# A two-layer graph kernel: a second queue fetches whole tiles of rows, 16 of them, for layer 1

## The chip, the cores and the metric

The kernel runs on one core of one Trainium2 chip. The metric is the device time of one execution in microseconds (us), as the median of several executions. A difference of less than 0.2%, about 7 us here, can't be told from no change.

## The reference

There are 12,500 nodes with 128 features each and 200,000 edges, sorted by their target node; every edge has one of 8 relations. Two layers are computed, and then a layer norm of the sum with the input:

```python
def _rgcn_conv(x, src, dst, et, basis, comp, root, bias):
    W = jnp.einsum('rb,bio->rio', comp, basis)
    xw = jnp.einsum('ni,rio->nro', x, W)
    msgs = xw[src, et]
    seg = dst * N_REL + et
    summed = jax.ops.segment_sum(msgs, seg, num_segments=N_NODES * N_REL)
    cnt = jax.ops.segment_sum(jnp.ones((msgs.shape[0],), x.dtype), seg, num_segments=N_NODES * N_REL)
    mean = summed / jnp.maximum(cnt, 1.0)[:, None]
    agg = mean.reshape(N_NODES, N_REL, HIDDEN).sum(axis=1)
    return agg + x @ root + bias
...
for l in range(N_LAYERS):
    h = jax.nn.relu(_rgcn_conv(h, src, dst, edge_type, basis[l], comp[l], root[l], bias[l])) + h
...
x = _layernorm(x + h, axis=-1)
```

## The kernel before

The edges are cut into 1,563 tiles of 128, and eight tiles make a quad; there are 196 quads. One turn of the main loop handles one quad, and the variable `o` counts the turns. The code numbers the layers 0 and 1; the text says layer 1 and layer 2. Nothing in the order of instructions is decided at run time: the program writes one list of operations, each engine takes its own in that order, and a wait is set where an operation needs the result or the buffer of another engine's.

Layer 1 first sums the rows of x by target and relation and multiplies by the weights afterwards. In turn `o` the following is written, in this order:

- GpSimd (POOL) fetches the rows of quad `o + 5`: one indirect DMA for each tile, 128 rows of 512 bytes (`gather`, line 806). The quads land in a ring of seven buffers `rows`, so the fetch of quad q + 7 has to wait until TensorE has read quad q. For the last six quads of the layer the fetch is only two turns ahead.
- TensorE (PE) multiplies each tile of rows with a one-hot matrix `dm` that VectorE (DVE) made: 16 instructions, line 1364, into the two banks `s` (`means`). Called M here.
- ScalarE (ACT) copies what is left from the turn before (`batch`, all at line 704): table halves (`y_row` out of the banks `pt` and `ct`), then the last product (`ys` out of `y`), then the new sums (`sT` out of `s`, two instructions). Behind them it issues stores that are due (`h_d`, `y_d`, line 701).
- `single_lists` and `single_rows` (lines 728 to 767) come next, see below.
- VectorE makes the one-hot matrices of quad `o + 2` and whatever other work is due.
- TensorE multiplies `sT` of quad `o - 1` with the eight relations' weights (`product`, line 1396, called P), adds the result into the accumulator of a node block (`place`, lines 1427 and 1429), and works on what else is due.

Three kinds of other work share the turns. In turns 0 to 42 the edge lists are turned and counted. From turn 50 on a table of h times the weights of layer 2 is made for every finished node block of 128 (`table`, line 1495, two halves a block). While more than four halves are waiting, one is made and copied by ScalarE within the turn (called T1), before TensorE may use the bank `pt` again for the next one (T2); a third, T3, goes to the bank `ct`. T2 and T3 are copied in the next turn's `batch`. By the program's lists the backlog is 51 halves at turn 50 and 6 at turn 75; after that T1 is made in the turns 76 to 80, 84 and 92. In turns 96 to 161 edges of layer 2 are sorted into groups on VectorE and TensorE with small copies and stores on ScalarE (`lo_d`, `sc_d`), and only one table half a turn is made; a backlog of 22 halves left by then goes in turns 162 to 176, again with T1 in each. Until turn 49 ScalarE copies `ys` in the same turn as P.

Layer 2 fetches rows of that table `y_d` by the same kind of indirect DMA, 1,067 tiles and 62 others; its fetches stand behind layer 1's in GpSimd's list, and the third quad of layer 2 waits until all of the table has been stored.

Some tiles of layer 1 aren't fetched by GpSimd. The list `SINGLES` names them: an issuing engine, the layer, and the tiles. Now there is one entry, SyncE's (SP) queue with every 56th tile from 191 on, 24 tiles. For such a tile the queue's engine issues 128 plain DMAs, one for each row. It does so in eight chunks of 16. In front of every second chunk it loads 32 row addresses from a list in memory into registers; the list `off_d` is written once, in turn 14, by one DMA of single 4-byte words. Every chunk has its place in the order of the turns (`single_rows`), before the turn that sums the tile:

```python
if (t - ts.step - 2 * Q + c * ts.step * RC // P) // Q != o:
    continue
...
return [by[e].dma_start(b[c * RC + j:c * RC + j + 1, :], bass.AP(
    tensor=t8.tensor, offset=offsets[e][a + j], ap=[[4 * D, 1], [1, 4 * D]]))
    for j in range(RC)]
```

Each engine in the list has two tile buffers `hw_<engine>`. GpSimd's `gather` leaves such tiles out, and M reads them from those buffers.

Of the kernel before, what the change touches and what calls it, by code (L numbers as in the profile page):

```python
# [430 lines left out]
def ordered_path(  # L431
# [38 lines left out]
    Q = 8  # L470
    NQ = -(-T // Q)
# [38 lines left out]
    NR = len(ROUTED)  # L510
    SORT = 96
    RC, RL = 16, 32
    SINGLES = [("SP", 0, range(191, NQ * Q - 80, 56))]
    SINGLE = {(l, t): (i, k) for i, (_, l, ts) in enumerate(SINGLES) for k, t in enumerate(ts)}
    LISTED = (14, NQ - 24)
    assert all(l == 0 or all(t // Q not in ROUTED and t // Q < NQ - 4 for t in ts) for _, l, ts in SINGLES)
    assert len(SINGLE) == sum(len(ts) for _, _, ts in SINGLES)
    assert D == P and R * K == P and B == BF + 1 and 1 < TL and LAST < P and BF % 4 == 0 and Q == G and N % 2 == 0
# [8 lines left out]
    def keep(shape, dtype, name):  # L527
        return const.tile(shape, dtype, name=name)
# [147 lines left out]

    hw_b = {e: [keep([P, D], F32, f"hw_{e}{i}") for i in range(2)] for e in {e: 0 for e, _, _ in SINGLES}}
    offs = [keep([P, len(ts)], I32, f"off{i}") for i, (_, _, ts) in enumerate(SINGLES)]
    off_d = [dram.tile([len(ts), P], I32, name=f"off_d{i}") for i, (_, _, ts) in enumerate(SINGLES)]
    by = {"SP": nc.sync, "ACT": nc.scalar}  # L680
# [1865 lines left out]
def kernel(  # L2546
# [18 lines left out]
    flag = ctx.enter_context(tc.tile_pool(name="flag", bufs=1))  # L2565
    bad = flag.tile([1, 1], I32, name="bad")
    plan = ordered_path(tc, bad, x, src, dst, et, basis, comp, root, bias, out)
    every = [mybir.EngineType.PE, mybir.EngineType.Activation, mybir.EngineType.DVE, mybir.EngineType.Pool,
             mybir.EngineType.SP]
# [36 lines left out]
```

## Time and profile before

| What | Value |
|---|---|
| time, median of 3 | 3384.41 us (3383.34 to 3385.06) |
| the profiled execution, its own time | 3385.05 us |
| its span, first to last instruction | 3383.1 us |
| granted TensorE clock, mean | 0.911 |
| PE busy | 2766.1 us (82%) |
| POOL busy | 2547.9 us (75%) |
| DVE busy | 2270.8 us (67%) |
| ACT busy | 644.9 us (19%) |
| layer 1's fetches on POOL | 4.6 to 1949.4 us |
| layer 2's fetches on POOL | 1950.6 to 3363.7 us |

Issuing a DMA isn't counted as busy time, so SP has no row here, and ACT's 19% holds only its copies. PE's busy time holds matmuls at both of its clock rates. A queue's issuing shows in rows that carry SPq, ACTq or POOLq.

### The profile page before, as it was taken

What the parts mean: (1) busy time and instruction counts of PE and PEld (TensorE: products, weight loads), DVE (VectorE), ACT (ScalarE), POOL (GpSimd) and SP (SyncE); (2) the same over time, 40 slices, a digit from 0 to 9 for tenths busy, and PEclk for the clock granted to TensorE, in tenths of its full rate; (3) what the DMA queues carried; (4) which work ended last, traced back from release to release, by engine and by line L of the source; (5) the groups of instructions that cost most, each with busy time, mean ns of one, the idle gap of its engine ahead of it and who ended that gap; (6) DMA issues with size and microseconds to landing.
All of it is one profiled execution on the core that took longest, in us unless ns stands there. A gap on an engine that the chain in (4) does not pass through costs nothing.

```text
span 3383.1 us, 73915 instructions
## 1 busy us (share of the span) xinstructions
PE 2766.1 (82%) x27537; PEld 2228.2 (66%) x27537; DVE 2270.8 (67%) x6302; ACT 644.9 (19%) x1627; POOL 2547.9 (75%) x2677
## 2 busy tenths in 40 slices
PE   6777667877667777777776739999999999999995
PEld 4565565656566666766565627777777777777774
DVE  6665454463367888888333238888888888888884
ACT  1211112222122222222222211111111111111110
POOL 7777777777777777777777777777777777777775
PEclk8999879888888888888988879999999999999997
DMA  4242223443322232222333232233223322333222
GB/s 138 56 59 64 57 77 113 132 130 95 89 82 81 75 89 76 82 77 82 115 105 89 88 101 73 72 84 85 78 78 84 84 78 78 84 85 82 78 78 61
DMA packets 171649, 289.03 MB, mean 85 GB/s; under 512 B 66163, under 2 KB 102813, under 8 KB 171285
## 3 DMA queue, kind: packets, MB, share of 16 engines
q0 software_dynamic: 85408, 175.09, 20.3%
q1 hardware_dynamic: 47146, 50.19, 5.0%
q10 hardware_dynamic: 38731, 58.99, 4.9%
q8 instruction: 218, 3.57, 0.5%
q14 instruction: 146, 1.20, 0.1%
HBM read 218.35 MB, written 65.70 MB: 84 GB/s over the span
## 4 chain that ended last, share of the span: by engine, by line
PE 43%; POOL 40%; issue 13%; DVE 2%; DMA 2%; ACT 1%; POOLq 0%; ACTq 0%; SPq 0%; DVEq 0%
POOL rows L806 40%; PE pt L1918 11%; PE y L1938 9%; PE po L1938 7%; PE po L1958 3%; PE s L2059 3%; PE ct L2026 2%; PE s L1364 2%; PE y L1396 1%; DMA rows<-in_x_dram,idx 1%; PE s L2061 1%; DVE dm L1270 1%; PE s L2063 1%; DVE arena L999 1%; PE pt L1495 0%
## 5 line engine op out<-in xcount | busy, mean ns | idle before, releaser
L806 POOL DMA_INDIRECT rows<-in_x_dram,idx x1539 | 1476.8, 960 | 471.3 <-issue 463.5
L806 POOL DMA_INDIRECT rows<-y_d,idy x1067 | 1010.4, 947 | 325.1 <-issue 316.6
L1364 PE MATMUL s<-dm,rows 128*128 128x128 f32 x3078 | 531.6, 344 | 379.6 <-DMA rows<-in_x_dram,idx 351.8
L1364 PEld LDWEIGHTS s<-dm,rows 128*128 128x128 f32 x3078 | 495.2, 252 | 441.1 <-issue 228.1
L1270 DVE TENSOR_SCALAR dm<-cols,kr,w 128x128 f32<-128x128 f16 x1563 | 525.1, 400 | 194.7 <-PE pt L1495 54.8
L1396 PE MATMUL y<-w_sb,sT 128*128 128x128 f32 x3136 | 438.6, 299 | 46.4 <-ACT sT L704 46.4
L1396 PEld LDWEIGHTS y<-w_sb,sT 128*128 128x128 f32 x3136 | 424.6, 217 | 56.4 <-ACT sT L704 55.2
L1918 PE MATMUL pt<-arena,dm 128*32 128x128 f32 x12152 | 391.3, 275 | 2.8 <-DVE dm L1868 2.1
L704 ACT ACTIVATE sT<-s 128x512 f32<-128x512 f32 x391 | 212.3, 594 | 824.8 <-PE s L1364 824.8
L1918 PEld LDWEIGHTS pt<-arena,dm 128*32 128x32 f32 x12152 | 324.6, 110 | 55.2 <-issue 43.0
L1938 PE MATMUL y<-arena,dm 128*128 128x304 f32 x620 | 229.6, 452 | 35.1 <-DVE arena L1885 35.1
L1229 DVE TENSOR_SCALAR sT<-cols,kr,w 128x32 f32<-128x32 f16 x1040 | 238.1, 300 | 7.4 <-PE s L2063 7.3
L1868 DVE TENSOR_TENSOR dm<-arena,cols 128x768 f32<-128x768 f16 x248 | 231.3, 933 | 4.1 <-DMA dm<-sc_d 3.7
L1448 DVE TENSOR_TENSOR po<-po,carry 128x128 f32<-128x128 f32 x98 | 28.8, 294 | 296.9 <-PE pt L1495 104.2
L1938 PE MATMUL po<-arena,dm 128*128 128x304 f32 x620 | 210.3, 421 | 0.0
L704 ACT ACTIVATE dm<-pt 128x256 f32<-128x256 f32 x248 | 95.4, 385 | 578.2 <-PE pt L1918 533.6
L1495 PE MATMUL pt<-w_sb,arena 128*128 128x512 f32 (+1 forms) x326 | 174.5, 618 | 26.3 <-ACT y_row L704 14.9
L704 ACT ACTIVATE y_row<-pt 128x512 f32<-128x512 f32 x165 | 98.5, 597 | 417.8 <-PE pt L1495 153.3
L1938 PEld LDWEIGHTS y<-arena,dm 128*128 128x128 f32 x620 | 102.9, 189 | 88.4 <-DVE arena L1885 35.3
L1885 DVE TENSOR_SCALAR arena<-cols,comp_sb 128x608 f32<-128x608 f16 x155 | 134.9, 902 | 36.1 <-DMA arena<-y_d,arena 36.0
L1938 PEld LDWEIGHTS po<-arena,dm 128*128 128x128 f32 x620 | 118.4, 191 | 41.3 <-issue 0.7
L1885 DVE TENSOR_SCALAR arena<-cols,sel 128x608 f32<-128x608 f16 x155 | 134.8, 902 | 0.0
(327 smaller groups left out, 3583.5 us busy)
## 6 DMA issues: line engine op xcount, KB each, us to landing
hw_SP<-in_x_dram SPq DMA_DIRECT2D x3072, 0.5 KB
y_d<-y_row ACTq DMA_DIRECT2D x96, 512.0 KB
rows<-in_x_dram,idx POOLq DMA_INDIRECT x1539
rows<-y_d,idy POOLq DMA_INDIRECT x1067
arena<-lo_d SPq DMA_DIRECT2D x62, 256.0 KB
x_g<-in_x_dram SPq DMA_DIRECT2D x24, 512.0 KB
h_d<-arena ACTq DMA_DIRECT2D x96, 64.0 KB
out_dram<-x_g SPq DMA_DIRECT2D x12, 512.0 KB
```

The lines of the kernel that those rows point to most:

```text
L704: act(lambda: nc.scalar.activation(out_t, in_t, AF.Copy), reads, writes)
L806: ins.append(nc.gpsimd.indirect_dma_start(out=t[:, i - q * Q, :], out_offset=None, in_=table_t, in_offset=bass.IndirectOffsetOnAxis(ap=ids ...
L1229: vec(in_turn([lambda i=i: nc.vector.tensor_scalar(t[:, i, :], cols[:, :2 * K], kr[:, i0 + i:i0 + i + 1], w[:, i0 + i:i0 + i + 1], op0=ALU ...
L1270: emits.append(lambda i=i: nc.vector.tensor_scalar(t[:, i - q * Q, :wide], cols[:, :wide], ids[:, i:i + 1], w[:, i:i + 1], op0=ALU.is_equa ...
L1364: last = nc.tensor.matmul(s_b[i // 4][0][:, i % 4, :], t[:, i, :] if one is None else one[0], d[:, i, :], start=True, stop=True)
L1396: last = nc.tensor.matmul(y[:m], t[:, r, :nt, :].rearrange("p t k -> p (t k)"), w_sb[:, 0, r, :], start=(r == 0), stop=(r == R - 1))
L1495: pe(lambda: nc.tensor.matmul(hb[:n].rearrange("p r d -> p (r d)"), hT[:, j * P:j * P + n], w_sb[:, 1, k * H:(k + 1) * H, :].rearrange("p ...
L1868: emits = [lambda: nc.vector.tensor_tensor(o[:, :3 * n].rearrange("p (j c) -> p j c", j=3), bits[:, None, u * n:(u + 1) * n].to_broadcast( ...
L1885: vec(lambda v=v, o=o: nc.vector.tensor_scalar(o, segs_p, sg[:, v:v + 1], sg[:, NTL + v:NTL + v + 1], op0=ALU.is_equal, op1=ALU.mult), ["n ...
L1918: last = nc.tensor.matmul(b[k * CAP:(k + 1) * CAP, x, :], o[:n, c:c + CAP], hT[:n, j * P:(j + 1) * P], start=jj == 0, stop=jj == SIZE[g] - 1)
L1938: last = nc.tensor.matmul(b.rearrange("p t d -> p (t d)")[:, :SEG], g[:, x * P:(x + 1) * P], o[:, k * SEG:(k + 1) * SEG], start=v == 0, st ...
L1958: pe(in_turn([lambda r=r: nc.tensor.matmul(b[:NW, 0, :], t_s[:, r * NW:(r + 1) * NW], w_sb[:, 1, r, :], start=r == 0, stop=r == R - 1) for ...
```

## The change

`SINGLES` gets a second entry: ScalarE's queue, layer 1, every 80th tile from 220 on, up to 1420. These are 16 tiles, none of them SP's. Everything else follows from the list: a second address list and its store to memory in turn 14 behind the first, two more tile buffers, 2,048 single-row DMAs and 64 address loads in ACT's order of instructions, 16 fewer indirect DMAs on POOL. ACT's chunks stand behind `batch` in the turns 15, 16, 18, 19, 20, 21, 23 and 24, and so on every ten turns up to turn 174; the first, third, fifth and seventh of a tile begin with the address load.

```diff
-    SINGLES = [("SP", 0, range(191, NQ * Q - 80, 56))]
+    SINGLES = [("SP", 0, range(191, NQ * Q - 80, 56)), ("ACT", 0, range(220, NQ * Q - 80, 80))]
```

## The prediction

> **What bounds the kernel now.** The page comes first, for the span and the costliest groups; then the fetch line by itself and what POOL waited for.
>
> ```profile
> span 3383.1 us, 73915 instructions
> ...
> L806 POOL DMA_INDIRECT rows<-in_x_dram,idx x1539 | 1476.8, 960 | 471.3 <-issue 463.5
> L806 POOL DMA_INDIRECT rows<-y_d,idy x1067 | 1010.4, 947 | 325.1 <-issue 316.6
> ```
> ```profile
> L806 POOL DMA_INDIRECT rows<-in_x_dram,idx x1539: 940/945/1986, 4.6 to 1949.4; - x193
> L806 POOL DMA_INDIRECT rows<-y_d,idy x1067: 940/945/1817, 1950.6 to 3363.7; - x178
> ```
> ```profile
> POOL rows L806 <- issue: 780.1, 2559, 0.3
> POOL rows L806 <- DMA arena<-in_dst_dram: 2.3, 1, 2.3
> ```
>
> POOL fetches without a break from 4.6 to 3363.7 us; its 780 us of idle time are 0.3 us behind each fetch, and the longest real wait is 2.3 us. So POOL sets the span in both layers, and its busy share of 75% hides that. A fetch in layer 1 costs 960 ns and 471.3/1539 = 306 ns of issue: 1.266 us. Ten turns after the change (80 tiles, less 80/56 = 1.43 of SP's and one of ACT's) are 77.6 fetches, 98.2 us: POOL's pace is 9.82 us a turn.
>
> **What goes.** Sixteen fetches, 16 x 1.266 = 20.2 us. If nothing else waits, that is the whole effect.
>
> **What comes: ACT's queue issues.** No row shows single rows on ACT; SP's rows are the nearest.
>
> ```profile
> L755 SPq TENSOR_LOAD <-off_d x2: 3655/3690/3726, 1008.1 to 1022.2; - x2
> ```
> ```profile
> L759 SPq DMA_DIRECT2D hw_SP<-in_x_dram x3072: 227/228/1083, 194.6 to 1773.1; - x192
> ```
> ```profile
> 1011.92 10.23 SPq L759 DMA_DIRECT2D hw_SP<-in_x_dram  x32
> ```
>
> From one address load to the next SP takes 14.1 us: 3.8 us of load, then 32 rows in 10.23 us, 0.32 us each. I take this for ACT too: a heavy chunk (load and 16 rows) is 9.0 us, a light one 5.1, a tile 56.4, all 16 tiles 902 us. ACT does its work in order, so copies behind a chunk wait for all of it. The lower bound is the issue time alone, 228 ns a row, 1.5 us off every chunk; a slower ACT is a rival below.
>
> Three smaller parts cost nothing that ends anywhere: the second list's store is one more issue of 0.37 us on SP, which then waits 19.4 us for the first list in any case (row below); VectorE makes that list with one more small instruction; and the same 512 bytes a row move as before, through another queue. M of such a quad waits for ACT's eight chunks too, the last of which is issued two or three turns ahead.
>
> **Where the copies wait.** POOL stops only when TensorE is six turns late, since the fetch of quad q + 7 waits for M of quad q. Now M begins as its rows land:
>
> ```profile
> 1003.50 0.94 POOL L806 DMA_INDIRECT rows<-in_x_dram,idx  x1 [0.30 <-issue]
> ...
> 1004.88 0.60 ACT L704 ACTIVATE y_row<-pt 128x512 f32<-128x512 f32 x1 [3.25 <-PE y L1706]
> ...
> 1005.37 0.63 ACT L704 ACTIVATE arena<-y 128x4 f32<-128x4 f32 x3
> ...
> 1006.03 0.28 ACT L704 ACTIVATE ys<-y 128x128 f32<-128x128 f32 x1
> ...
> 1006.06 1.80 PE L1364 MATMUL s<-dm,rows 128*128 128x128 f32 x14 [1.22 <-ACT arena L704]
> ...
> 1008.13 0.34 ACTq L701 DMA_DIRECT2D y_d<-y_row  x1
> ...
> 1008.99 0.77 ACTq L701 DMA_DIRECT2D sc_d<-arena  x1
> ```
>
> A quad's last fetch ends at 1004.44 and its M starts at 1006.06, 1.6 us later. TensorE may thus fall 6 x 9.82 - 1.6 - 2.7 (its M) = 54 us behind before POOL waits once. I follow this lag through the stages.
>
> Turns 15 to 49. The second address list lands late, and the chunk of turn 15 waits for it with all of ACT behind it.
>
> ```profile
> L701 SPq DMA_DIRECT2D off_d<-off x1: 370/370/370, 170.5 to 170.5; - x1
> ```
> ```profile
> SPq L755 <- DMA off_d<-off: 19.4, 1, 19.4
> ```
> ```profile
> 182.79 0.60 ACT L704 ACTIVATE sT<-s 128x512 f32<-128x512 f32 x1 [3.67 <-PE s L1364]
> ```
> ```profile
> 228.79 1.95 PE L1364 MATMUL s<-dm,rows 128*128 128x128 f32 x16
> 231.91 2.05 PE L1396 MATMUL y<-w_sb,sT 128*128 128x128 f32 x16 [1.17 <-ACT sT L704]
> ...
> 236.44 2.05 PE L1364 MATMUL s<-dm,rows 128*128 128x128 f32 x16 [0.53 <-DMA rows<-in_x_dram,idx]
> ```
>
> The first list, 24 x 128 words, was issued at 170.5 and landed about 190. The second has 16 x 128, by that rate 13 us more: about 203, while ACT stands at turn 15 from 184. So 19 us of wait, and TensorE is some 14 us late there anyway (first wait for rows at 236). A turn without a row wait is 7.2 us (228.79 to 235.9). A heavy chunk here lies beside P, its followers and the next M: 0.4 + 9.0 + ys 0.3 + sT 1.1 = 10.8 a turn, a light one 7.5. Ten turns are 4 x 10.8 + 4 x 7.5 + 2 x 7.2 = 88 against 98. The 42 us of lag (19, 14 and the chunk) shrink by some 8 per ten; the edge lists' turns 22 to 25 and 39 to 42, where TensorE waits for ACT's copies behind the chunk, give part of it back. I carry 15 us into turn 50, bounds 0 and 40.
>
> Turns 50 to 76: here the chunk is not covered. T2 needs T1's copy, and that stands behind the chunk.
>
> ```profile
> 599.62 2.68 PE L1364 MATMUL s<-dm,rows 128*128 128x128 f32 x16 [2.75 <-DMA rows<-in_x_dram,idx]
> 602.09 3.00 PE L1396 MATMUL y<-w_sb,sT 128*128 128x128 f32 x16
> 604.92 1.02 PE L1495 MATMUL pt<-w_sb,arena 128*128 128x512 f32 x2
> ...
> 606.63 1.13 PE L1495 MATMUL pt<-w_sb,arena 128*128 128x512 f32 x2
> 607.60 1.02 PE L1495 MATMUL ct<-w_sb,arena 128*128 128x512 f32 x2
> 610.47 3.24 PE L1364 MATMUL s<-dm,rows 128*128 128x128 f32 x16 [1.86 <-DMA rows<-in_x_dram,idx]
> ...
> 619.80 1.95 PE L1364 MATMUL s<-dm,rows 128*128 128x128 f32 x16
> ...
> 629.82 3.75 PE L1364 MATMUL s<-dm,rows 128*128 128x128 f32 x16 [3.91 <-DMA rows<-in_x_dram,idx]
> ```
> ```profile
> 602.33 0.60 ACT L704 ACTIVATE sT<-s 128x512 f32<-128x512 f32 x1 [4.17 <-PE s L1364]
> 602.40 0.33 ACTq L701 DMA_DIRECT2D h_d<-arena  x1
> 602.76 0.45 ACTq L701 DMA_DIRECT2D y_d<-y_row  x1
> ...
> 605.98 0.60 ACT L704 ACTIVATE y_row<-pt 128x512 f32<-128x512 f32 x1 [2.56 <-PE pt L1495]
> ```
>
> M ends at 602.3, the stores take 0.7 us on average, then the chunk. Behind it come T1's copy (0.65), T2 and T3 (2.0), the next M (1.95). TensorE has work until 4.3 us after M's end (606.6), so it idles 6.0 us in a heavy turn and 2.1 in a light one. M took 3.75 us after 3.91 idle and 3.24 after 1.86, against 1.95: I add 1.8 and 1.3. A heavy turn is 0.7 + 9.0 + 0.65 + 2.0 + 1.95 + 1.8 = 16.1 us, a light one 11.7, one without a chunk 8. Of the 27 turns 11 are heavy, 11 light, 5 free: 177 + 129 + 40 = 346 us, POOL's pace 265. The lag grows by 81; with 15 it would be 96, so POOL waits 96 - 54 = 42 us.
>
> By the Trainium skill, TensorE: Matmul & The Clock Gate, Part 1: The HAM clock gate, the clock halves only after an idle window of about 3.4 us, so light turns would stay at full speed, and the sum would come out 16 x 1.3 = 21 us lower, 3414 us. The 3.24 us after 1.86 us idle speak for the higher price.
>
> Turns 77 to 95: T1 still in 78 to 80, so 8 + 16.1 + 11.7 + 16.1 = 52 in four turns against 39: 12 us more of waiting. Without T1 a heavy turn is copies 0.9, sT and stores 0.8, chunk 9.0: 10.7, a light one about 7. The lag comes down to some 40.
>
> Turns 96 to 161: the three groups of copies before sT end 1.43 us after they begin (1004.88 to 1006.31), stores until 1.5 us after sT, then the chunk: 11.9 heavy, 8.4 light (TensorE's chain), 8.2 free. Ten turns 97.6, POOL's pace 98.2: no change. Bounds: minus 10 and, with TensorE's clock low, plus 5 for every ten.
>
> Turns 162 to 174: T1 again, 5 heavy, 5 light, 3 free: 163 against 128. Lag 35 + 35 = 70, so POOL waits 16 us. From 175 on there are no chunks; at 7 us a turn TensorE gains 2.8, 54 us in 19 turns, and the table is ready about when POOL needs it.
>
> **Sum.** -20 + 42 + 12 + 16 = +50. The profiled execution took 3385.05 us, 0.6 over the median; the forecast is 3435 us.
>
> **Rivals.**
> The ring covers it (faster). If turns 50 to 76 take no more than 265 + 54 - 15 = 304 us (heavy 13.9, light 10.1), POOL never waits there. Without the clock's 1.8 and 1.3 us they are 14.3 and 10.4, so the clock has to stay up and a chunk be 0.4 us cheaper, or the lag at turn 50 be 0; at the lower bound of 228 ns a row they are 14.6 and 10.2 with the clock's part, 312 us in all and next to no wait. Then 3385 - 20 = 3365. For it: from 236 us on TensorE waits for rows, so it has time to give. Against: the chain T1, chunk, T2 is written into the order.
>
> Break-even. POOL's waits come to 13 to 27 us: 3378 to 3392.
>
> One generator for both queues (much slower). If ACT's issue had to wait while SP's runs, two at 228 ns would alternate, 0.456 us a row instead of 0.32: 2.2 us more for each of 128 chunks, 280 us, of which the covered turns 15 to 49 (28 chunks) hide most: about 3435 + 210 = 3645.
>
> ```profile
> L701 ACTq DMA_DIRECT2D h_d<-arena x96: 325/327/1228, 110.9 to 1946.5; - x96
> ```
> ```profile
> L701 SPq DMA_DIRECT2D jmp<-h_d x32: 319/320/320, 2035.2 to 3308.3; - x32
> ```
>
> Against it: ACT's stores took 327 ns while SP was issuing most of the time, SP's of the same size 320 when ACT issued none. The Trainium skill, Perfetto Trace Analysis, DMA Instruction — HWDGE (DVE, Sync), says that the generator is locked for exclusive use while it makes descriptors; by that rule this case holds if the two queues share one, and these two rows speak against it.
>
> **How the numbers follow.** POOL waits clearly more than it saves 0.57; ring covers 0.27; break-even 0.08; one generator 0.08. So faster 0.27, same 0.08, slower 0.65. The likeliest case's own range is 3392 to 3530: its upper end takes lag 40 at turn 50 (+25), plus 5 for every ten turns of the sort (+35), a chunk dearer by 0.4 us (+15) and a late table (+20). The range for 8 in 10 goes from 3364 to 3530.
>
> **What would show it.** Right: ACT rows about 0.32 us apart with loads near 3.8; POOL's fetch line waiting for PE, first about turns 65 to 75 (fetches of 640 to 760 us), again before the end of layer 1; M no longer waiting for rows; T2 behind a chunk; layer 2 as long as before. Wrong: POOL's waits still all issue, or ACT's rows far from 0.32 us.

## The result, and the profile after

The changed kernel takes 3442.08 us (median of 5, 3437.1 to 3443.3) against 3383.95 us before (3383.15 to 3385.06), a ratio of 1.017 with a 95% interval of 1.0156 to 1.0183. The forecast was 3435 us, so its sign and its likeliest case held, and the sum was 7 us short; part of that closeness is luck, as the account of the prediction below shows. The profiled execution of the changed kernel spans 3438.1 us at a mean granted clock of 0.897.

First the fetch line by itself (count, duration in ns as least, median and most, first and last start in us):

```profile
L806 POOL DMA_INDIRECT rows<-in_x_dram,idx x1523: 938/944/1887, 4.7 to 2007.6; - x191
L806 POOL DMA_INDIRECT rows<-y_d,idy x1067: 940/944/1814, 2008.8 to 3421.7; - x178
```

Layer 1 is 58 us longer (2007.6 for 1949.4) although it has 16 fetches less. Layer 2 takes 1412.9 us from first to last fetch, as against 1413.1 before: all of the loss lies in layer 1. Next, what POOL waited for (us in total, times, longest):

```profile
POOL rows L806 <- issue: 770.1, 2525, 0.3
POOL rows L806 <- PE s L1364: 86.6, 24, 8.9
...
POOL rows L806 <- DMA arena<-in_dst_dram: 2.5, 1, 2.5
```

The second line is new. M, TensorE's means, holds back 24 fetches. Of the 86.6 us, 0.3 us each would have been issue anyway: 86.6 - 24 x 0.3 = 79.4 us. Less the 20.2 us of the fetches saved, that is +59 us, against 58 us between the two medians. The same line asked for one stretch at a time, 500 to 640, 640 to 780, 780 to 900 and 900 to 960 us:

```profile
POOL rows L806 <- PE s L1364: 1.7, 1, 1.7
```
```profile
POOL rows L806 <- PE s L1364: 33.1, 7, 8.9
```
```profile
POOL rows L806 <- PE s L1364: 38.3, 8, 8.0
```
```profile
POOL rows L806 <- PE s L1364: 12.0, 3, 6.8
```

After 960 us only five of 0.3 us are left, the length of an issue. So POOL stands in the table's turns and nowhere else. What makes M late shows in TensorE's timeline of two turns, a heavy and a light one (start, duration, and in brackets the idle time before and what ended it):

```profile
639.99 1.72 PE L1364 MATMUL s<-dm,rows 128*128 128x128 f32 x14
...
643.97 1.02 PE L1495 MATMUL pt<-w_sb,arena 128*128 128x512 f32 x2
...
653.24 2.07 PE L1495 MATMUL pt<-w_sb,arena 128*128 128x512 f32 x2 [7.81 <-ACT y_row L704]
...
655.96 2.92 PE L1364 MATMUL s<-dm,rows 128*128 128x128 f32 x16
...
660.51 1.02 PE L1495 MATMUL pt<-w_sb,arena 128*128 128x512 f32 x2
...
666.18 2.08 PE L1495 MATMUL pt<-w_sb,arena 128*128 128x512 f32 x2 [4.00 <-ACT y_row L704]
668.05 1.92 PE L1495 MATMUL ct<-w_sb,arena 128*128 128x512 f32 x2
669.75 2.86 PE L1364 MATMUL s<-dm,rows 128*128 128x128 f32 x16
```

ScalarE's timeline of the same two turns shows what T2 waited for (the address load's time is not a row here; it lies between 643.1 and 646.8):

```profile
642.47 0.59 ACT L704 ACTIVATE sT<-s 128x512 f32<-128x512 f32 x1
646.81 5.68 ACTq L759 DMA_DIRECT2D hw_ACT<-in_x_dram  x16
652.59 0.60 ACT L704 ACTIVATE y_row<-pt 128x512 f32<-128x512 f32 x1 [9.53 <-issue]
...
659.97 5.46 ACTq L759 DMA_DIRECT2D hw_ACT<-in_x_dram  x16
665.53 0.60 ACT L704 ACTIVATE y_row<-pt 128x512 f32<-128x512 f32 x1 [5.53 <-issue]
```

T1 is ready at 645.0, and ScalarE copies it at 652.59, when its 16 issues are out; T2 begins 0.65 us later. ScalarE "idles" 9.53 us in that gap by the trace's count, while its sequencer has no free moment. The first M after the chunk starts 16.0 us after the one before, the second 13.8.

### The profile page after: what moved, and what is told of

Its sections match the earlier page's. It is cut to its first block, busy times and chain, and to the rows that moved or that the text cites. A ratio compares the mean times of both kernels' runs of the same rounds, so it can differ in the third digit from the quotient of the medians.

```text
span 3438.1 us, 78120 instructions
## 1 busy us (share of the span) xinstructions
PE 2736.8 (80%) x27537; PEld 2182.4 (63%) x27537; DVE 2268.3 (66%) x6303; ACT 639.0 (19%) x1627; POOL 2531.0 (74%) x2661
## 4 chain that ended last, share of the span: by engine, by line
PE 57%; ACTq 16%; issue 8%; DVE 7%; POOL 6%; ACT 4%; DMA 2%; POOLq 0%; SPq 0%; DVEq 0%
ACTq L759 11%; PE pt L1918 10%; PE y L1938 8%; PE po L1938 7%; PE s L1364 7%; PE y L1396 6%; POOL rows L806 6%; ACTq L755 4%; PE pt L1495 3%; PE po L1958 3%; PE s L2059 3%; PE ct L2026 2%; DVE dm L1270 2%; ACT sT L704 2%; ACTq L701 1%
## 5 line engine op out<-in xcount | busy, mean ns | idle before, releaser
L806 POOL DMA_INDIRECT rows<-in_x_dram,idx x1523 | 1460.1, 959 | 546.2 <-issue 452.8
L1396 PE MATMUL y<-w_sb,sT 128*128 128x128 f32 x3136 | 462.7, 310 | 251.5 <-ACT ys L704 163.0
L1396 PEld LDWEIGHTS y<-w_sb,sT 128*128 128x128 f32 x3136 | 434.4, 221 | 269.3 <-ACT ys L704 172.1
L1364 PEld LDWEIGHTS s<-dm,rows 128*128 128x128 f32 x3046 | 413.4, 214 | 70.4 <-issue 64.1
L1364 PE MATMUL s<-dm,rows 128*128 128x128 f32 x3046 | 427.7, 298 | 25.4 <-DMA rows<-in_x_dram,idx 24.5
L1495 PE MATMUL pt<-w_sb,arena 128*128 128x512 f32 (+1 forms) x326 | 202.3, 707 | 171.9 <-ACT y_row L704 155.2
L1938 PE MATMUL po<-arena,dm 128*128 128x304 f32 x620 | 210.3, 421 | 0.0
L1495 PEld LDWEIGHTS pt<-w_sb,arena 128*128 128x128 f32 (+1 forms) x326 | 60.3, 220 | 189.6 <-ACT y_row L704 168.0
```

What stands on the lines that cost most here:

```text
L806: ins.append(nc.gpsimd.indirect_dma_start(out=t[:, i - q * Q, :], out_offset=None, in_=table_t, in_offset=bass.IndirectOffsetOnAxis(ap=ids ...
L1364: last = nc.tensor.matmul(s_b[i // 4][0][:, i % 4, :], t[:, i, :] if one is None else one[0], d[:, i, :], start=True, stop=True)
L1396: last = nc.tensor.matmul(y[:m], t[:, r, :nt, :].rearrange("p t k -> p (t k)"), w_sb[:, 0, r, :], start=(r == 0), stop=(r == R - 1))
L1495: pe(lambda: nc.tensor.matmul(hb[:n].rearrange("p r d -> p (r d)"), hT[:, j * P:j * P + n], w_sb[:, 1, k * H:(k + 1) * H, :].rearrange("p ...
L1938: last = nc.tensor.matmul(b.rearrange("p t d -> p (t d)")[:, :SEG], g[:, x * P:(x + 1) * P], o[:, k * SEG:(k + 1) * SEG], start=v == 0, st ...
```

## The experiments

Each group shares its runs of the kernel before. Theory: the issues stand in ScalarE's order ahead of T1's copy; TensorE loses time in turns 50 to 80 until its lag exceeds the ring of `rows`, and then POOL stands. In the first group the kernel before took 3387.05 us (3384.84 to 3391.66).

**T1's copy on VectorE.** It takes the one dependent copy away from behind the chunk and leaves all issues in place.

```diff
-            b()
-            plan.mark("ACT")
+            b(vcopy)
+            plan.mark("DVE")
```

> All 16 tiles stay on ScalarE's queue; only the copy of T1 (the table half that is copied within the turn) goes from ScalarE to VectorE, so that T2 no longer waits for a copy that stands behind a chunk. If the loss comes from that order, a heavy turn of the table stage falls from about 16.4 us to ScalarE's own 11.3 (copies 1.5, sums and stores 0.8, chunk 9.0), ten turns are about 97 us against POOL's 98, POOL never waits and the time is 3384 - 20 = 3364 us. If the issues cost by themselves (their traffic, their place on ScalarE in every stage, the late address list), it stays near 3440.

Measured: 3368.24 us, ratio 0.9942 (0.9925 to 0.9958): faster than the kernel before by about what 16 fetches are worth (3387.05 - 20.2 = 3366.9), where the change is slower than it. POOL's waits for M in it:

```profile
POOL rows L806 <- PE s L1364: 1.2, 4, 0.3
```

All 2,048 issues are still on ScalarE. It is their place before T1's copy that costs, not their presence. VectorE's copy can hardly be a gain in itself: in the kernel before POOL sets the time and never waits for M, so an earlier copy has nothing to shorten; a control on another chip stands further down. One thing of the expectation missed: ten turns of the table stage take 106 us (287.5 for the 27 turns 50 to 76) and not 97, so TensorE's lag still grows there, from 21.7 us at turn 50 to 42.1 at turn 77, and stays within the 54 that the ring allows.

**The chunk at the end of the turn.** ScalarE's chunk is written behind the turn's other work instead of right behind `batch`.

```diff
-        single_rows(0, o)
+        single_rows(0, o, "SP")
...
         plan.mark("PE")
+        single_rows(0, o, "ACT")
```

> All 16 tiles; ScalarE's chunk moves from behind the sums' copies to the end of the turn, behind T1's copy. T2 is then free of the chunk, but the next turn's P waits for the copy of y behind it, and T1 follows P: 9.0 + 1.5 + P and T1 3.1 + copy 0.65 = 14.3 us for a heavy turn, 10.4 for a light one. Turns 50 to 76 come to some 312 us and up to 330 with the clock, POOL's waits to 18 to 36 us: 3382 to 3400. If only the one wait of T2 mattered, it would be 3364; if the place in the turn doesn't matter, 3440.

Measured: 3494.18 us, ratio 1.0312 (1.0295 to 1.033): missed, it is worse than the change. POOL's waits for M, over the whole execution and in the first 500 us, where the change had none:

```profile
POOL rows L806 <- PE s L1364: 145.7, 48, 10.4
```
```profile
POOL rows L806 <- PE s L1364: 25.3, 14, 4.7
```

TensorE's timeline of two turns of it:

```profile
648.55 1.95 PE L1364 MATMUL s<-dm,rows 128*128 128x128 f32 x16
656.65 3.78 PE L1396 MATMUL y<-w_sb,sT 128*128 128x128 f32 x16 [6.15 <-ACT ys L704]
660.22 1.91 PE L1495 MATMUL pt<-w_sb,arena 128*128 128x512 f32 x2
...
664.64 1.95 PE L1364 MATMUL s<-dm,rows 128*128 128x128 f32 x16
668.76 3.48 PE L1396 MATMUL y<-w_sb,sT 128*128 128x128 f32 x16 [2.17 <-ACT ys L704]
```

T1 is no longer behind the chunk, but the next turn's copies of `ys` and `sT` are, and P needs them. Every turn has those, so POOL now also waits in the turns ahead of the table stage. It doesn't in every stage: after 1100 us no wait is longer than 0.3 us. The heavy turn is as long as in the change (16.1 us from M to M). My expectation named this wait for `ys`, but its sum had 3.1 us for P and T1, which take 3.78 and 1.91 us in the heavy turn shown, and it left out that the turns before 50 pay as well.

**Where in the layer the tiles lie.** Two kernels keep parts of the list: nine tiles whose chunks lie outside the turns 45 to 94, and the five whose chunks lie inside them.

```diff
-("ACT", 0, range(220, NQ * Q - 80, 80))
+("ACT", 0, range(220, 381, 80)), ("ACT", 0, range(860, 1261, 80))
```
```diff
-("ACT", 0, range(220, NQ * Q - 80, 80))
+("ACT", 0, range(460, 781, 80))
```

> Nine of the 16 tiles: those whose chunks lie in the turns 15 to 44 and 95 to 154, none in the table stages. If the loss is made in the turns 50 to 80 alone, the nine fetches are saved and nothing waits: 3384 - 11.4 = 3373 us. If each tile costs its share of the 58 us on top of everything, it is 3384 + 33 = 3417.

> Five of the 16 tiles: those whose chunks lie in the turns 45 to 94. By the lag's account they make nearly all of the loss: the lag grows by 23, 29 and 37 us in the three ten-turn stretches from turn 47 on as before, only the 17 us or so that it brought along from the earlier turns are missing. POOL's waits are then about 62 us instead of 79 and the time 3384 - 6 + 62 = 3440 us. If each tile costs its share, it is 3384 + 18 = 3402.

Measured: the nine outside 3375.55 us, 0.9962 (0.9948 to 0.9976); the five inside 3435.28 us, 1.0141 (1.012 to 1.0163). POOL's waits for M in the first, then in the second:

```profile
POOL rows L806 <- PE s L1364: 0.3, 1, 0.3
```
```profile
POOL rows L806 <- PE s L1364: 59.3, 16, 7.7
```

Both add up: 9 x 1.266 = 11.4 us saved gives 3375.7; 59.3 - 16 x 0.3 - 5 x 1.266 = +48.2 gives 3435.3 (the one execution that these waits are from took 3431.61 us). A third of the issues makes most of the loss, and nine tiles' issues in the other stages cost nothing. That refutes any price per issue or per byte that is the same in all stages. The two tiles of the turns 155 to 174 are in neither kernel; in the change POOL doesn't wait in those turns.

**Half the issues, the same bytes.** Each issue brings two rows, the second a repeat of the first, so every second row of those tiles is wrong. In this group the kernel before took 3386.05 us.

```diff
+                        if e == "ACT":
+                            return [by[e].dma_start(b[c * RC + j:c * RC + j + 2, :], bass.AP(
+                                tensor=t8.tensor, offset=offsets[e][a + j], ap=[[0, 2], [1, 4 * D]]))
+                                for j in range(0, RC, 2)]
```

> The changed kernel with ScalarE's 16 issues of a tile made into 8, each of two rows of which the second repeats the first (so every second row of those tiles is left wrong). Same bytes for the queue, same fetches taken from POOL, half the time in ScalarE's order. Theory (the time that the issues take in ScalarE's order is what costs): a heavy turn falls by some 2.7 us, so that the lag of TensorE reaches the ring late or not at all: 3364 to 3370 us, up to 3415 if it still reaches it. Rival (the bytes or the queue of ScalarE cost, not the issues): 3442.

Measured: 3365.44 us, ratio 0.9936 (0.9919 to 0.9953), which is 3386.05 - 20.2 = 3365.8. POOL waits for M three times, 0.3 us each, an issue's length:

```profile
POOL rows L810 <- PE s L1368: 0.9, 3, 0.3
```

The same heavy and light turn as shown for the change, 58 and 59, first on TensorE and then the chunks on ScalarE (in this kernel TensorE's lines are numbered 4 higher, and ScalarE's issues are line 760):

```profile
591.05 1.72 PE L1368 MATMUL s<-dm,rows 128*128 128x128 f32 x14
...
601.70 2.08 PE L1499 MATMUL pt<-w_sb,arena 128*128 128x512 f32 x2 [5.62 <-ACT y_row L704]
...
604.42 2.00 PE L1368 MATMUL s<-dm,rows 128*128 128x128 f32 x16
...
611.62 1.12 PE L1499 MATMUL pt<-w_sb,arena 128*128 128x512 f32 x2 [1.90 <-ACT y_row L704]
612.59 1.02 PE L1499 MATMUL ct<-w_sb,arena 128*128 128x512 f32 x2
613.44 1.95 PE L1368 MATMUL s<-dm,rows 128*128 128x128 f32 x16
```
```profile
598.08 2.87 ACTq L760 DMA_DIRECT2D hw_ACT<-in_x_dram  x8
...
607.46 3.41 ACTq L760 DMA_DIRECT2D hw_ACT<-in_x_dram  x8
```

The chunks' issues are 2.8 us shorter in the heavy turn and 2.1 in the light one. From M to M the heavy turn falls by 2.6 us (13.4 for 16.0), the light one by 4.8 (9.0 for 13.8): with T2's wait down from 4.00 to 1.90 us, TensorE keeps its full rate too (T2 1.12 for 2.08 us, T3 1.02 for 1.92). In this light turn the gain is larger than the time taken out, because the clock stays up. Over turns 50 to 76 the averages are 13.7 us heavy and 9.9 us light, from 16.5 and 12.4 in the change; they hold waits for rows too, 210.3 us in all of the layer, since TensorE now catches up with POOL:

```profile
L1368 PE MATMUL s<-dm,rows 128*128 128x128 f32 x3046 | 483.1, 323 | 229.1 <-DMA rows<-in_x_dram,idx 210.3 <-issue 7.5 <-ACT ys L704 6.3
```

**One quad more in the ring.** The fetch runs six turns ahead, with a ring of eight quads. That is a whole turn, 9.82 us of lag, and not the half of one that the expectation's text says; the sum of about 10 us is meant for it. The kernel before took 3380.69 us.

```diff
-    AHEAD = 5
+    AHEAD = 6
```

> The changed kernel with the fetches half a turn further ahead (AHEAD 6 for 5, and the buffers that go with it). Theory (POOL stands because TensorE's lag exceeds what the ring of buffers allows): the allowed lag grows once by half a turn, some 5 to 10 us, so that of the 59 us that POOL lost, about 10 go once: 3432 us where the change gave 3442, with POOL's first wait a few turns later. Rival (the ring has no part in the waits): 3442. Rival (a little more room gives back all of it): 3364 to 3384.

Measured: 3432.09 us (3423.54 to 3441.32), ratio 1.0153 (1.0126 to 1.0179). The times can't tell this from the change's 1.017 (1.0156 to 1.0183). The trace leans to the theory, though weakly: POOL's waits for M are fewer and 4.8 us shorter (80.6 - 20 x 0.3 = 74.6 against 79.4), half of the 9.8 that the theory gives, and the first begins later. First waits of the change, then of the deeper ring:

```profile
635.11 0.94 POOL L806 DMA_INDIRECT rows<-in_x_dram,idx  x1 [1.65 <-PE s L1364]
...
659.16 0.95 POOL L806 DMA_INDIRECT rows<-in_x_dram,idx  x1 [5.63 <-PE s L1364]
```
```profile
664.30 0.94 POOL L806 DMA_INDIRECT rows<-in_x_dram,idx  x1 [1.89 <-PE s L1364]
```

So a little more room doesn't give the loss back; that rival falls. That the ring's size has a part in it is likely, but not shown by a time.

**On two other chips.** There the kernel before took 4992 us and 5003 us, with a mean granted clock of 0.79 to 0.80. The trace of the last kernel in the table below puts idle times of ScalarE, VectorE and GpSimd down to something remote, which the traces above hardly show (on ScalarE 1208.9 us before one group of copies), so these runs say nothing on the sums in us. The changed kernel itself wasn't run there.

| Kernel | us | ratio (95%) |
|---|---|---|
| ring of eight | 5158.11 | 1.033 (1.0268 to 1.0391) |
| ring of eight, second chip | 5166.96 | 1.0323 (1.0296 to 1.0349) |
| half the issues | 5041.59 | 1.0103 (1.0037 to 1.017) |
| half the issues, second chip | 5042.09 | 1.0068 (1.0046 to 1.009) |
| lists made earlier | 5133.34 | 1.0275 (1.0209 to 1.034) |
| before, T1 copied by VectorE | 4995.09 | 1.0005 (0.9978 to 1.0033) |

The first four were meant as the two experiments above, with these expectations:

> The changed kernel with a ring of eight row buffers instead of seven (fetches six turns ahead). If POOL's waits are the lag less what the ring allows, one buffer more takes one turn, 9.8 us, off them: 3442 - 10 = 3432 us. If the loss were issue or transfer time on ScalarE's queue itself, the ring wouldn't matter: 3442.

> The changed kernel with two more buffers for fetched rows (the fetches run one tile of half a turn further ahead). Theory (the lag of TensorE exceeds what the ring allows): the allowed lag grows by half a turn of about 10 us, so 10 us of the 59 us goes once: about 3432 us where the change gave 3442. Rival (the waits are of another kind, and the ring has no part in them): 3442. Rival (more room gives back all): 3384.

> The changed kernel with half as many issues in a chunk: eight DMAs that put one row of x into two partitions each, so that every second row of such a tile holds its neighbour's row. A chunk gets 2.65 us shorter (8 x 0.34 minus little), a heavy turn of the table stage 13.7 us instead of 16.4 and a light one 10.8 instead of 13.4. Ten turns there are then 107 us instead of 128 against POOL's 98, the lag grows by some 27 from 20, under the 54 that the ring allows, and POOL doesn't wait: 3364 to 3370 us. If the cost were in proportion to the issues, half of the loss of 78 would stay: 3384 - 20 + 39 = 3403.

> The changed kernel with ScalarE's 16 issues of a tile made into 8, each of them two rows of which the second repeats the first (so every second row of those tiles is left wrong). Same bytes for the queue, same fetches taken from POOL, half the time in ScalarE's order. Theory (the time that the issues take in ScalarE's order is what costs): the heavy turn falls by some 2.7 us, the lag by turn 80 by about 2.7 times 16 divided over the turns up to there, some 20 to 30 us of the 59 us and with less lag at turn 50 also no reaching of the ring for long: 3364 to 3415 us, nearer the lower end. Rival (the transfers or the queue cost, not the issues): 3442.

The other two are the change with `LISTED = (10, NQ - 24)` for `(14, NQ - 24)`, and the kernel before with only the edit of T1's copy:

> The changed kernel with both address lists written in turn 10 instead of 14, so that ScalarE's first chunk no longer waits for its list (it stood from 191 to 202 us). The lag at turn 50 was 25 us; 10 to 19 of them come from that wait, and since the lag hardly shrinks in turns 15 to 50, the time falls by that: 3423 to 3432 us. If the turns 15 to 50 would have won the time back anyway, it stays at 3442.

> The kernel before, with T1's copy on VectorE and no tiles on ScalarE's queue: the control of the first experiment. POOL sets the span and never waits for TensorE here, so the order of the copies is worth nothing: 3384 us, no difference. If that edit were a gain by itself, the kernel would be as fast as the first experiment's, about 3368.

The control is the one that can be read: T1's copy on VectorE changes nothing where no issues stand before it, on such a chip at least. Here even the control's POOL waits for M:

```profile
POOL rows L806 <- PE s L1364: 332.7, 63, 42.8
```

So TensorE holds POOL up there before any chunk is added. The three kernels with 16 issues before T1's copy took 2.8 to 3.3% more and the two with 8 took 0.7 to 1.0% more; the order is the same as above, but no run there shows that the place of the issues is the cause. What the earlier lists are worth stays open.

## Why the prediction was right, point by point

**POOL's saving, 20.2 us.** Right. Three kernels without waits of POOL for M come out within 1.4 us of the kernel before less 1.266 us for each fetch taken away.

**The chunk.** Nearly right. Rows of ScalarE's queue and of SyncE's in the changed kernel:

```profile
L755 ACTq TENSOR_LOAD <-off_d x64: 3607/3842/4688, 201.6 to 1847.1; - x64
```
```profile
L759 SPq DMA_DIRECT2D hw_SP<-in_x_dram x3072: 227/228/1057, 205.5 to 1869.8; - x192
...
L759 ACTq DMA_DIRECT2D hw_ACT<-in_x_dram x2048: 231/235/771, 205.4 to 1863.2; - x187
```

An issue takes 235 ns, SyncE's 228, and 16 of them 5.1 to 5.7 us in the timelines, about 0.34 us a row for 0.32. The first load at 201.6 us stands where I had put it (203). What is written ahead of T1's copy was a little too short as well: in the light turn shown, M ends at 658.9 us and ScalarE's copy of T1 starts at 665.53, 6.7 us later, where I had 0.7 + 5.1 = 5.8.

**Turns 50 to 76, 42 us.** This is the step that failed in size. POOL waited 1.7 + 33.1 + 38.3 less 16 x 0.3, that is 68 us, up to 900 us, when turn 77 begins. The smaller part of the error, 10.7 of 26 us, is the lag at turn 50. Quad 50's last fetch and its M:

```profile
505.74 0.94 POOL L806 DMA_INDIRECT rows<-in_x_dram,idx  x1 [0.30 <-issue]
```
```profile
534.00 2.27 PE L1364 MATMUL s<-dm,rows 128*128 128x128 f32 x14
...
894.09 1.91 PE L1364 MATMUL s<-dm,rows 128*128 128x128 f32 x8
```

The fetch ends at 506.7, M could start 1.6 us later and starts at 534.0: a lag of 25.7 us, where I took 15 (bounds 0 to 40). By the same reckoning the lag was 32.2 us at turn 17 and 32.4 at turn 27, where I had started from 42. In turns 27 to 37 it shrank by 7 us, close to the 8 that I had for ten turns. In 37 to 47, with the edge lists' turns 39 to 42 among them, it grew by as much again; I had named that and given it no number. The larger part is the turns' length, 14 us. From M(50) to M(77) are 360.1 us, where I had 346. By M's starts a heavy turn takes 16.5 us on average, a light one 12.4 and a free one 8.4 (11, 11 and 5 of them), for 16.1, 11.7 and 8. The light turns make half of that, 11 x 0.7: in the one shown T2 waits 4.00 us where I expected TensorE to idle 2.1, and then T2 and T3 run at half rate, 2.08 and 1.92 us. POOL's first wait, at 635 us, came just ahead of the 640 to 760 us that I had named. With both corrections the prediction's own sum is 25.7 + 360.1 - 265 - 54 = 67 us, against 68 measured.

The Trainium skill, TensorE: Matmul & The Clock Gate, Part 1: The HAM clock gate, puts the loss of the clock at an idle window of about 3.4 us. The trace agrees for T2 (half rate after 4.00 us of idle, full rate after 1.90), but in the kernel with the chunk at the end P took 3.48 us after 2.17 us of idle, against 1.95, and the granted clock was 1.00 from 665.7 to 669.1 us and 0.50 from 669.2 to 672.5. The measurement decides: 3.4 us of idle is no safe bound, and the length of the wait alone doesn't settle it, since a T2 of the change kept its full rate (1.12 us) after 2.64 us. The lower sum of 3414 us that I worked out by the page did not come, and the case it spoke of, idle times of 2.1 us, hardly arose: in eight of the eleven light turns the wait behind the chunk was 3.5 to 5.3 us.

**Turns 77 to 95, 12 us.** Right: 12.0 - 3 x 0.3 = 11.1 us between 900 and 960.

**Turns 96 to 161, no change.** Off on the good side: the lag fell. M of tiles that came by ScalarE's queue, in turns 97 and 157:

```profile
1080.22 0.39 PE L1364 MATMUL s<-dm,hw_ACT 128*128 128x128 f32 x2
...
1659.80 0.39 PE L1364 MATMUL s<-dm,hw_ACT 128*128 128x128 f32 x2
```

That is 96.6 us for ten turns (97.6 predicted), while POOL's own pace over the same quads was 99.7 instead of 98.2. By the same reckoning as at turn 50, the lag fell from 34.3 us at turn 97 to 15.5 at turn 157 and 9.6 at turn 162, where I had left it at 35. It thus fell by about 4 us for every ten turns, within the bound of minus 10 that I had given; why POOL's fetches came slower there isn't shown.

**Turns 162 to 174, 16 us.** Wrong: POOL didn't wait. The last fetches of quads 162 and 175, and M of the same quads:

```profile
1691.42 0.94 POOL L806 DMA_INDIRECT rows<-in_x_dram,idx  x1 [0.30 <-issue]
...
1817.76 0.94 POOL L806 DMA_INDIRECT rows<-in_x_dram,idx  x1 [0.30 <-issue]
```
```profile
1703.59 1.95 PE L1364 MATMUL s<-dm,rows 128*128 128x128 f32 x16
...
1865.18 1.95 PE L1364 MATMUL s<-dm,rows 128*128 128x128 f32 x16
```

The turns themselves came out as forecast: 161.6 us from M(162) to M(175), where I had 163, so that the lag grew by 35 us, as I had it. But it grew from 9.6 to 44.9 us and not from 35 to 70, and 44.9 is below 54. This step failed because the one before it did.

So +50 was -20 + 42 + 12 + 16, and the runs say -20 + 68 + 11 + 0 = +59. Two errors of 26 and 16 us of opposite sign hid each other in part. The mechanism and the stage were right and the sizes of two terms were not, so it is luck in part that the forecast came within 7 us.

**The rivals.** "The ring covers it" fell for the change, but the reckoning behind its threshold, 304 us for turns 50 to 76 at a lag of 15, held. With each kernel's own lag at turn 50 the threshold is 319 us with half the issues (lag 0), 297 with T1's copy on VectorE (21.7) and 293 in the change (25.7). Those turns took 297.8, 287.5 and 360.1 us, and only in the change did POOL wait for M longer than an issue's 0.3 us. "One generator for both queues" fell: SyncE's issues are 228 ns as before and ScalarE's 235, not twice that. While ScalarE issued the 16 of the heavy turn shown, from 646.8 to 652.5 us, SyncE's went on at their usual length:

```profile
L759 SPq DMA_DIRECT2D hw_SP<-in_x_dram x18: 227/228/228, 646.6 to 652.1; - x18
```

The Trainium skill, Perfetto Trace Analysis, DMA Instruction — HWDGE (DVE, Sync), has the generator locked for one user at a time; no such waiting between the two queues shows in these rows.

## What to carry to other kernels

An engine with a busy share of 19% had no room in its order at one place: 16 DMA issues and an address load are over 9 us in which nothing behind them runs, and no busy time shows it. Before issues go on an engine that also computes, look stage by stage at which instruction stands behind them, who waits for it, and how much lag the buffers in between allow; the remedy was to move that one copy to another engine, which turned +1.7% into -0.6%. Moving the issues to the end of the turn only changed which copy was late.

## What the runs showed of the hardware

An engine's sequencer can be the limit while the engine counts as idle: 9.53 us of ScalarE's idle time before one copy was "issue". A wait of 4.00 us on TensorE cost about 2.8 us more in what followed (T2 2.08 for 1.12, T3 1.92 for 1.02, M 2.86 for 1.95), so taking 2.1 us of issues out of the light turn shown gave 4.8 us back. And the kernel before took 48% more on two other chips, with TensorE's mean granted clock near 0.8.
